# A recommender's GRU kernel: a bf16 count of the sequences alive, and one product that puts the last results in place

## The chip, the cores and the metric

The kernel runs on one core of a Trainium2 chip. The core has five engines that work at the same time, each through its own list of instructions in order: TensorE (PE in the profile; PEld is its loading of weights), VectorE (DVE), ScalarE (ACT), GpSimd (POOL) and SyncE (SP, which here only starts DMAs). They wait for each other through semaphores. TensorE writes to PSUM, which has eight banks; the other data lie in SBUF, in 128 partitions. The metric is the time of one execution on the device in microseconds; a smaller one is better.

## The reference

For B = 1024 sequences of T = 100 steps, with vectors of 128 numbers, the reference computes:

```python
hist_sum = (item_historical_embedding * fmask[:, :, None]).sum(1) / sequential_length[:, None]
_, gru_seq = jax.lax.scan(gru_step, h0, jnp.swapaxes(item_historical_embedding, 0, 1))
keys = jnp.swapaxes(gru_seq, 0, 1)
feat = jnp.concatenate([keys, q, keys - q, q * keys], axis=-1)
score = _mlp(feat, [...], relu)                       # then masked, softmax over the steps
pooled = jnp.einsum('bt,btd->bd', attn, keys)
att_seq = pooled.T[:T]
_, aug_seq = jax.lax.scan(augru_step, h0, (jnp.swapaxes(keys, 0, 1), att_seq))
attention_feature = aug_seq at step sequential_length - 1 of each sequence
comb = [user, item, hist_sum, item * hist_sum, attention_feature]
scores = _mlp(comb, [...], sigmoid)                   # 640 -> 200 -> 80 -> 1
return scores[:, 0]
```

So there are two recurrences of 100 steps, one after the other: a GRU, and a second one (AUGRU) whose update gate is scaled by an attention weight. A sequence needs the second one only as far as its own length.

## The kernel before, in words

**First phase** (`gru_phase`): per step t the two halves of 512 sequences are done one after the other (method `gru`, L577 to L637), then the attention network of the step before (`attend`, L761). Beside this goes a list of small jobs, the generator `load_later`, which moves on by one piece per step, after the gates of that step. It ranks the sequences by length. One of its pieces counts how many sequences are alive at each step: `alive` (L336) is 1 where the length is over the step, as a 128 x 8 x 100 tile, and eight products with a column of ones (L353 to L356) add it up over the partitions into `count`, in PSUM. From `count` VectorE works out `over` (L359 to L370), which chooses between three versions of the second phase with narrower or full widths. The products stand in TensorE's list between the gates of a step and the `attend` of the step before it.

**Second phase** (`augru_phase`): the sequences are sorted by length, so that at step t only the first `widths[t]` columns of each half are worked on (264 at t = 50, 260 at t = 51, 44 at the end). `half_step` (L1279) does one half of one step: products that close the gates with the state (L1268) and open those of the half that follows (L1264), on VectorE the new state and the reset state `r` (L1298, L1300, L1302, L1305, L1308) and the transpose of a key that is needed two steps later (L1253). The two halves alternate, so that one half's VectorE and ScalarE work lies under the other's products. When the width is 72 or less, `whole_step` does both halves at once.

As sequences end, `predict(g)` computes the final network for group g of 128 sorted sequences, in pieces spread over the steps, and writes its 128 results to `early_d` in DRAM with an indirect DMA. The last group, g = 0, ends only at t = 99, so its work is the tail of the kernel, and its results don't go through DRAM. They are put in place by a product: `last_places` (L1505), called once at the end of step t = 50 (`HALF_TIME`, L1582), makes for each of the 128 sequences a row that is 1 at its own index and 0 elsewhere (an iota of 512 and a comparison, twice, both on GpSimd). In the tail four products with the column y repeated 32 times (L1494 to L1502), one for each quarter of the 1024 results, put quarter q on the partitions 32 q to 32 q + 31. VectorE adds this to `all_y` (L1503), which holds the results of the other groups, fetched by `earlier_results` (L1521) from `early_d` and repeated on 32 partitions each. The last DMA (L1630) stores the rows of the partitions 0, 32, 64 and 96.

**What sets the order.** Both phases have a manual schedule: each engine's instructions stand in the order in which the code makes them, and the semaphores follow from the tiles that an instruction reads and writes. A tile that one engine still reads isn't written by another before that read is done, and a tile from a pool with two buffers waits for the readers of the tile two before it. PSUM banks of the second phase are handed out in turn by `bank` (L1176) from a ring of seven.

Of the kernel before, what the change touches and what calls it, by code (L numbers as in the profile page):

```python
# [9 lines left out]
F32 = mybir.dt.float32  # L10
BF16 = mybir.dt.bfloat16
I32 = mybir.dt.int32
U8 = mybir.dt.uint8
AF = mybir.ActivationFunctionType
ALU = mybir.AluOpType
AX = mybir.AxisListType
# [3 lines left out]
P = 128  # L20
B = 1024
T = 100
HB = 512
NH = B // HB
NG = B // P
GH = HB // P

R = 32
# [3 lines left out]
M0, M1 = 200, 80  # L32
# [48 lines left out]
BQ = B // (P // R)  # L81
# [4 lines left out]
def kernel(ctx: ExitStack, tc: tile.TileContext, a: dict, out: bass.AP):  # L86
# [26 lines left out]
    nc = tc.nc  # L113
# [16 lines left out]
    early_d = dram.tile([B, 1], F32, name="early_d")  # L130
# [7 lines left out]
    ident = const.tile([P, P], F32, name="ident")  # L138
    item = const.tile([P, B], F32, name="item")
    hist = const.tile([P, B], F32, name="hist")  # L140
    pooled = const.tile([P, NK, R], F32, name="pooled")
# [1 line left out]
    idx_k = const.tile([P, KH, NH], I32, name="idx_k")  # L143
    quad = const.tile([P, SOON], F32, name="quad")
    used_s = const.tile([P, NH, GH, T - SOON], U8, name="used_s")
    all_y = pooled.rearrange("p k r -> p (k r)")[:, :BQ]
    idx_p = const.tile([P, HB // PR], I32, name="idx_p")
    h_all = const.tile([P, NH, HB], F32, name="h_all")
    h3 = [h_all[:, i, :] for i in range(NH)]
    mid = ctx.enter_context(tc.tile_pool(name="mid", bufs=2))  # L150
# [3 lines left out]
    later = {}  # L154
# [49 lines left out]
    def gru_phase(pools):  # L204
# [11 lines left out]
        pre = pools.enter_context(tc.tile_pool(name="pre", bufs=1))  # L216
# [60 lines left out]
        def load_later():  # L277
# [55 lines left out]
                nc.scalar.copy(room[-1], room_i)  # L333
            yield

            alive = mid.tile([P, NG, T], F32, name="alive", **once)  # L336
            nc.vector.tensor_tensor(
                out=alive,
                in0=length.unsqueeze(2).to_broadcast([P, NG, T]),
                in1=step.unsqueeze(1).to_broadcast([P, NG, T]),  # L340
                op=ALU.is_gt,
            )
            ones = pre.tile([P, 1], F32, name="ones")
            nc.gpsimd.memset(ones, 1.0)
            rlen = pre.tile([P, NG], F32, name="rlen")
            nc.vector.reciprocal(rlen, length)
# [806 lines left out]
    def augru_phase(pools, widths, alive):  # L1153
# [260 lines left out]
        def predict(g, last=False):  # L1414


            m0, m1 = later["m0"], later["m1"]
            n = M0 // MC
            tag = "last" if last else "a"

            def of_pool(name):
                return bank(name) if last else pa.tile([P, HB], F32, tag="a", name=name)


            def rows_of(out_ap, in_ap, o, i):
                nc.gpsimd.indirect_dma_start(
                    out=out_ap,
                    out_offset=o and bass.IndirectOffsetOnAxis(ap=idx_p[:, g : g + 1], axis=0),
                    in_=in_ap,
                    in_offset=i and bass.IndirectOffsetOnAxis(ap=idx_p[:, g : g + 1], axis=0),  # L1430
                )

            part = sp.tile([P, M0], F32, tag=f"part_{tag}", name="part3")
            rows_of(part, part_d, None, True)
            yield
            f0 = sp.tile([MC, n, P], F32, name="f0")
            if last:
                p0 = [of_pool("p0")[:MC, :P] for _ in range(n)]
                for j in range(n):
                    nc.tensor.matmul(  # L1440
                        p0[j], lhsT=part[:, ts(j, MC)], rhs=ident, start=True, stop=False
                    )
                yield
                for j in range(n):
                    nc.tensor.matmul(
                        p0[j].rearrange("p (i r) -> p i r", i=NH),
                        lhsT=m0[:, 4, ts(j, MC)],
                        rhs=h_all[:, :, ts(g, PR)],
                        start=False,
                        stop=True,  # L1450
                    )
            else:
                state = sp.tile([P, NH, PR], F32, name="state3")
                nc.scalar.copy(state, h_all[:, :, ts(g, PR)])
                yield
                p = of_pool("rows")[:, :M0]
                nc.tensor.matmul(
                    p,
                    lhsT=state.rearrange("p i r -> p (i r)"),
                    rhs=m0[:, 4, :],  # L1460
                    start=True,
                    stop=True,
                )
                yield
                nc.vector.tensor_add(part, p, part)
                yield
                p = of_pool("p0")
                p0 = [p[:MC, ts(j, P)] for j in range(n)]
                for j in range(n):
                    nc.tensor.transpose(p0[j], part[:, ts(j, MC)], ident)  # L1470
            yield
            for j in range(n):
                nc.scalar.activation(
                    f0[:, j, :], p0[j], AF.Sigmoid, bias=later["c0"][:, j : j + 1]
                )
            yield
            p1 = of_pool("p1")[:M1, :P]
            for j in range(n):
                nc.tensor.matmul(  # L1479
                    p1, lhsT=m1[:, j, :], rhs=f0[:, j, :], start=(j == 0), stop=(j == n - 1)  # L1480
                )
            yield
            f1 = sp.tile([M1, P], F32, name="f1")
            nc.scalar.activation(f1, p1, AF.Sigmoid, bias=later["c1"])
            yield
            p2 = of_pool("p2")[:, 0:1]
            nc.tensor.matmul(p2, lhsT=f1, rhs=later["m2"], start=True, stop=True)
            yield
            y = sp.tile([P, 1], F32, name="y")
            nc.scalar.activation(y, p2, AF.Sigmoid, bias=later["c2"])  # L1490
            if not last:
                rows_of(early_d, y, True, None)
                return
            p = of_pool("po")[:, :BQ]  # L1494
            for q in range(P // R):
                nc.tensor.matmul(
                    p[ts(q, R), :],
                    lhsT=y.to_broadcast([P, R]),
                    rhs=later["places"][q // 2][:, ts(q % 2, BQ)],
                    start=True,  # L1500
                    stop=True,
                )  # L1502
            nc.vector.tensor_add(all_y, p, all_y)  # L1503

        def last_places():  # L1505
            own = sp.tile([P, 1], F32, name="own3", bufs=1)
            nc.gpsimd.tensor_copy(own, idx_p[:, 0:1])
            later["places"] = []
            for i in range(NH):
                row = wp.tile([P, HB], F32, tag="att_r", name="places", bufs=2)  # L1510
                nc.gpsimd.iota(
                    row,
                    pattern=[[1, HB]],
                    base=i * HB,
                    channel_multiplier=0,
                    allow_small_or_imprecise_dtypes=True,
                )
                nc.gpsimd.tensor_scalar(row, row, own, None, ALU.is_equal)
                later["places"].append(row)

        def earlier_results():  # L1521
            nc.sync.dma_start(
                out=all_y,
                in_=early_d.rearrange("(q c) o -> q (o c)", c=BQ)
                .unsqueeze(1)
                .to_broadcast([P // R, R, BQ]),
            )

        def gathers(q):
# [92 lines left out]
    with none.Else():  # L1622
# [6 lines left out]
                augru(2)  # L1629
    nc.sync.dma_start(  # L1630
        out=out.rearrange("(q c) -> q c", c=BQ),
        in_=all_y.rearrange("(q r) c -> q r c", r=R)[:, 0, :],
    )


# [64 lines left out]
```

## Time and profile before

| | us |
|---|---|
| median of 3 timed runs | 2016.64 (2015.94 to 2016.9) |
| profiled execution, first to last instruction (span) | 1995.2 |
| median less span | 21.4 |
| PE busy in the span | 1980.5 |
| DVE busy | 1673.4 |
| POOL busy | 1262.7 |
| ACT busy | 940.7 |

The profile records one execution with its span; for that execution no other time is given, so its time as a whole is the span and what lies around it, and the median of the timed runs stands beside it. A line of a timeline gives the start and the duration in us, the engine, the line of the kernel, the operation, what is written and read, the shapes, and in brackets how long the engine stood idle before and what ended this. In the lists of groups the last columns are the busy time in us with the mean of one instruction in ns, and the idle time before them. The rows of a view by windows give, for each stretch, its length and the busy time of PE, PEld, DVE, ACT and POOL with the number of instructions, then the clock that TensorE was granted (1.00 is full speed), the DMA engines' busy share and the GB/s. An fp32 product shows as two records on PE and two on PEld.

### The profile page before, as it was taken

The page shows a single profiled execution, that of the slowest core. Times are in us where ns is not written, and L with a number is a line of the kernel's source. Part 1 is how long each engine was busy: PE and PEld are TensorE (multiplying, and loading weights), DVE is VectorE, ACT ScalarE, POOL GpSimd, SP SyncE. Part 2 cuts the span into 40 slices and gives each one's busy share as a digit, 9 for nine tenths or more (in the row PEclk, how much of TensorE's full clock was granted, in tenths as well). Part 3 has the DMA queues.
Part 4 walks back from the last instruction along what each step waited for, and adds up shares of the span by engine and source line. Part 5 has one row for each costly group of instructions (what it writes and reads, how often), then busy time and mean ns, then how long its engine had stood idle before and what let it go on. Part 6 is the DMA issues. An engine that isn't in the chain of part 4 may idle for free.

```text
span 1995.2 us, 40926 instructions
## 1 busy us (share of the span) xinstructions
PE 1980.5 (99%) x15324; PEld 877.7 (44%) x15324; DVE 1673.4 (84%) x3036; ACT 940.7 (47%) x1689; POOL 1262.7 (63%) x1300
## 2 busy tenths in 40 slices
PE   9999999999999999999999999999999999999998
PEld 2333333333333333333333333334444556678997
DVE  7888999887979898888888798998687778888995
ACT  4444454454544444544545444446334444445553
POOL 0333939669796959496796858898763354445331
PEclk9999999999999999999999999999999999999999
DMA  4443333223334434332343333332543333333331
GB/s 125 99 119 92 108 105 102 89 84 108 116 104 113 116 99 134 111 106 85 103 129 108 93 107 108 92 108 67 155 146 92 96 111 97 93 103 100 83 81 35
DMA packets 244572, 205.59 MB, mean 103 GB/s; under 512 B 61811, under 2 KB 207068, under 8 KB 244364
## 3 DMA queue, kind: packets, MB, share of 16 engines
q1 hardware_dynamic: 231852, 170.31, 29.5%
q0 software_dynamic: 12224, 32.05, 5.7%
q8 instruction: 122, 2.00, 0.4%
q14 instruction: 86, 0.70, 0.1%
q10 hardware_dynamic: 288, 0.52, 0.1%
HBM read 146.75 MB, written 54.42 MB: 101 GB/s over the span
## 4 chain that ended last, share of the span: by engine, by line
PE 98%; DVE 1%; ACT 0%; issue 0%; ACTq 0%; DVEq 0%
PE ps L588 51%; PE pm L770 18%; PE ph L1268 5%; PE pr L1264 4%; PE pu L1264 4%; PE ph L1264 4%; PE pu L1268 4%; PE pr L1268 4%; PE last L737 1%; PE pr L1359 0%; PE ph L1359 0%; PE p L1479 0%; ACT pr L1378 0%; PE pd L248 0%; DVE r L1386 0%
## 5 line engine op out<-in xcount | busy, mean ns | idle before, releaser
L588 PE MATMUL ps<-x,wih 128*32 128x512 f32 x4800 | 603.2, 593 | 0.0
L588 PE MATMUL ps<-hn,whh 128*32 128x512 f32 x4752 | 597.1, 592 | 0.0
L588 PEld LDWEIGHTS ps<-x,wih 128*32 128x32 f32 x4800 | 175.6, 110 | 342.7 <-issue 338.1
L588 PEld LDWEIGHTS ps<-hn,whh 128*32 128x32 f32 x4752 | 173.7, 110 | 338.2 <-issue 335.6
L600 ACT ACTIVATE r<-ps,brz 128x512 f32<-128x512 f32 x200 | 137.5, 688 | 381.3 <-PE ps L588 381.1
L573 POOL TENSOR_TENSOR xm<-x,m 128x512 f32<-128x512 f32 x200 | 233.3, 1167 | 66.7 <-DMA m<-mask_d 66.5
L574 POOL TENSOR_TENSOR hist<-hist,xm 128x512 f32<-128x512 f32 x200 | 258.2, 1291 | 15.7
L193 POOL DMA_INDIRECT rows<-keys_d,idx_k x218 | 212.0, 972 | 84.0 <-POOL rows L192 69.2
L700 POOL TENSOR_TENSOR pooled<-pooled,kw 128x512 f32<-128x512 f32 x192 | 245.5, 1279 | 15.1
L699 POOL TENSOR_TENSOR kw<-kt,e 128x512 f32<-128x512 f32 x192 | 206.3, 1074 | 67.9 <-DVE e L888 67.9
L621 ACT ACTIVATE ps<-ps,bih 128x512 f32<-128x512 f32 x198 | 131.1, 662 | 228.4 <-DVE ps L618 228.4
L770 PE MATMUL pm<-hn,wk 128*32 128x512 f32 x1200 | 215.0, 592 | 0.0
L770 PE MATMUL pm<-kq,wkq 128*32 128x512 f32 x1200 | 214.9, 592 | 0.0
L1276 ACT ACTIVATE c<-ph,bh 128x510 f32<-128x510 f32 (+57 forms) x174 | 88.3, 507 | 252.0 <-PE ph L1268 251.5
L608 DVE SCALAR_TENSOR_TENSOR u<-ps,bhh,r 128x512 f32<-128x512 f32 x198 | 147.4, 744 | 68.5 <-PE ps L588 66.3
L770 PE MATMUL pm<-mv,w 128*32 128x512 f32 (+1 forms) x808 | 194.9, 592 | 0.1
L631 DVE TENSOR_TENSOR d<-hn,ps 128x512 f32<-128x512 f32 x198 | 136.0, 687 | 36.0 <-ACT ps L621 35.7
L618 DVE TENSOR_TENSOR ps<-ps,u 128x512 f32<-128x512 f32 x200 | 140.0, 700 | 24.1 <-PE ps L588 3.1
L642 ACT COPY hn<-ps 128x512 f32<-128x512 f32 x198 | 115.4, 583 | 92.5 <-DVE kq L637 90.8
L632 DVE TENSOR_TENSOR d<-ps,d 128x512 f32<-128x512 f32 x198 | 136.9, 691 | 26.2 <-ACT ps L622 11.0
L192 POOL COPY rows<-rest 128x1 f32<-128x1 f32 x186 | 35.0, 188 | 192.8 <-DVE rest L1308 191.1
L1298 DVE TENSOR_TENSOR pu<-pu,c 128x510 f32<-128x510 f32 (+57 forms) x173 | 81.9, 473 | 77.8 <-ACT c L1276 75.5
(271 smaller groups left out, 3138.9 us busy)
## 6 DMA issues: line engine op xcount, KB each, us to landing
x<-in_hist_x SPq DMA_DIRECT2D x210, 256.0 KB
keys_d<-kt SPq DMA_DIRECT2D x48, 1024.0 KB
m<-mask_d SPq DMA_DIRECT2D x200, 128.0 KB
rows<-keys_d,idx_k POOLq DMA_INDIRECT x218, 3.0
s_b<-mv SPq DMA_DIRECT2D x200, 8.0 KB
keys_d<-kt SPq DMA_DIRECT2D x32, 64.0 KB
mask_i<-in_mask SPq DMA_DIRECT2D x8, 200.0 KB
part_d<-part SPq DMA_DIRECT2D x2, 400.0 KB
```

The source lines that it names most:

```text
L193: nc.gpsimd.indirect_dma_start(out=r[:, at, :], out_offset=None, in_=keys_d[q], in_offset=bass.IndirectOffsetOnAxis(ap=idx_k[:, k, i : i + ...
L573: nc.gpsimd.tensor_mul(d, x, m)
L574: nc.gpsimd.tensor_add(acc, acc, d)
L588: nc.tensor.matmul(p[ts(q, R), :], lhsT=w[:, g, ts(q, R)], rhs=v, start=(j == 0), stop=(j == len(parts) - 1),)
L600: nc.scalar.activation(r, pr, AF.Sigmoid, bias=brz[:, 0:1])
L608: nc.vector.scalar_tensor_tensor(out=u, in0=ph, scalar=bhh[:, 2:3], in1=r, op0=ALU.add, op1=ALU.mult,)
L618: nc.vector.tensor_add(pi, pi, u)
L699: eng.tensor_mul(d, k, w)
L700: eng.tensor_add(acc, acc, d)
L770: nc.tensor.matmul(p[i][s, :], lhsT=w[:, s], rhs=v, start=start, stop=stop)
L1264: nc.tensor.matmul(p, lhsT=m[:, 1, :], rhs=k, start=True, stop=False)
L1268: nc.tensor.matmul(p, lhsT=m[:, 0, :], rhs=v, start=False, stop=True)
```

## The change

Two things change. The tile `alive` and the column of ones for the count become bf16. And the last results are placed by one product in place of four. For this, `last_places` makes four rows of 256 instead of two of 512; VectorE takes the maximum of each (1 where the sequence's index lies in that quarter) into a column of `others`, and GpSimd adds the four rows into one, `places`, which is row 0 itself. `others` is then (it - 1) x 1e30: 0 in the sequence's own quarter, -1e30 in the three others. In the tail the product for p2 becomes one of four columns: it is opened with identity x `others` before the last state is known, and closed with the network's last layer in all four columns, so that after the sigmoid y is the result in its own quarter's column and 0 in the others. One product of y (128 x 4) with `places` (128 x 256) gives 4 x 256 results. `all_y` has four partitions in place of 128, and the DMA that fills it and the one that stores it change with it. The order in which the banks go to p1 and p2 of the last group changes, since p2 is now opened first.

```diff
-    all_y = pooled.rearrange("p k r -> p (k r)")[:, :BQ]
+    all_y = pooled.rearrange("p k r -> p (k r)")[: B // BQ, :BQ]
...
-            alive = mid.tile([P, NG, T], F32, name="alive", **once)
+            alive = mid.tile([P, NG, T], BF16, name="alive", **once)
...
-            ones = pre.tile([P, 1], F32, name="ones")
+            ones = pre.tile([P, 1], BF16, name="ones")
...
+                p2 = of_pool("p2")[:, : B // BQ]
+                nc.tensor.matmul(p2, lhsT=ident, rhs=later["others"], start=True, stop=False)
                 yield
...
+            if last:
+                nc.tensor.matmul(
+                    p2,
+                    lhsT=f1,
+                    rhs=later["m2"].to_broadcast([M1, B // BQ]),
+                    start=False,
+                    stop=True,
+                )
+                y = sp.tile([P, B // BQ], F32, name="y4", bufs=1)
+                nc.scalar.activation(y, p2, AF.Sigmoid, bias=later["c2"])
+                p = of_pool("po")[: B // BQ, :BQ]
+                nc.tensor.matmul(p, lhsT=y, rhs=later["places"], start=True, stop=True)
+                nc.vector.tensor_add(all_y, p, all_y)
+                return
...
-            p = of_pool("po")[:, :BQ]
-            for q in range(P // R):
-                nc.tensor.matmul(
-                    p[ts(q, R), :],
-                    lhsT=y.to_broadcast([P, R]),
-                    rhs=later["places"][q // 2][:, ts(q % 2, BQ)],
-                    start=True,
-                    stop=True,
-                )
-            nc.vector.tensor_add(all_y, p, all_y)
...
-            later["places"] = []
-            for i in range(NH):
-                row = wp.tile([P, HB], F32, tag="att_r", name="places", bufs=2)
+            others = later["others"] = sp.tile([P, B // BQ], F32, name="others", bufs=1)
+            places = later["places"] = sp.tile([P, BQ], F32, name="places", bufs=1)
+            for q in range(B // BQ):
+                row = places if q == 0 else wp.tile([P, HB], F32, tag="att_r", name="row3", bufs=2)[:, :BQ]
                 nc.gpsimd.iota(
                     row,
-                    pattern=[[1, HB]],
-                    base=i * HB,
+                    pattern=[[1, BQ]],
+                    base=q * BQ,
                     channel_multiplier=0,
                     allow_small_or_imprecise_dtypes=True,
                 )
                 nc.gpsimd.tensor_scalar(row, row, own, None, ALU.is_equal)
-                later["places"].append(row)
+                nc.vector.tensor_reduce(others[:, q : q + 1], row, AX.X, ALU.max)
+                if q:
+                    nc.gpsimd.tensor_add(places, places, row)
+            nc.vector.tensor_scalar(others, others, 1.0, 1e30, ALU.subtract, ALU.mult)
...
-                in_=early_d.rearrange("(q c) o -> q (o c)", c=BQ)
-                .unsqueeze(1)
-                .to_broadcast([P // R, R, BQ]),
+                in_=early_d.rearrange("(q c) o -> q (o c)", c=BQ),
...
-        in_=all_y.rearrange("(q r) c -> q r c", r=R)[:, 0, :],
+        in_=all_y,
```

More of the change, by code (lines that the diff above doesn't have):

```diff
@@ L1490, in predict @@
             nc.scalar.activation(y, p2, AF.Sigmoid, bias=later["c2"])
-            if not last:
-                rows_of(early_d, y, True, None)
-                return
-            p = of_pool("po")[:, :BQ]
-            for q in range(P // R):
-                nc.tensor.matmul(
-                    p[ts(q, R), :],
-                    lhsT=y.to_broadcast([P, R]),
-                    rhs=later["places"][q // 2][:, ts(q % 2, BQ)],
-                    start=True,
-                    stop=True,
-                )
-            nc.vector.tensor_add(all_y, p, all_y)
+            rows_of(early_d, y, True, None)
         def last_places():
```

## The prediction

> **What bounds the kernel now.** I read the page first, then the windows by stage, then the chain around the three places that the diff touches.
>
> ```profile
> span 1995.2 us, 40926 instructions
> PE 1980.5 (99%) x15324; PEld 877.7 (44%) x15324; DVE 1673.4 (84%) x3036; ACT 940.7 (47%) x1689; POOL 1262.7 (63%) x1300
> PE 98%; DVE 1%; ACT 0%; issue 0%; ACTq 0%; DVEq 0%
> ```
>
> TensorE is busy for 99% of the span, and 98% of the chain that ended last lies on it. So time that the change takes off TensorE counts in full, and so does time in which it makes TensorE wait. The span is 1995.2 us; the median of the timed runs is 2016.64 us, so 21.4 us lie outside the span. The change touches nothing there, and I add the sum to the median. About 0.2%, 4.0 us here, is what a measurement of this kernel can tell from no change: over 2020.67 is slower, under 2012.6 faster.
>
> **The count.** The chain and the waits there:
>
> ```profile
> 119.94 1.27 PE count L354 x15
> 121.21 0.26 issue
> 121.47 0.25 PE count L354
> DVE ps L618 <- PE ps L588: 3.1, 1, 3.1
> ```
>
> Eight fp32 products show as 16 records and hold the chain for 1.27 + 0.26 + 0.25 = 1.78 us. The trace has no bf16 product. Cost from above: as now, no gain. From below: one record per product and each shorter. The pitch of the records is (1.27 + 0.25 - 0.25) / 15 = 0.085 us; one record in place of two leaves 8 x 0.085 = 0.68 and takes away 0.68; if the gap of 0.26 goes too and the passes are shorter still, up to 1.35 goes. But the last row is a warning: VectorE waited 3.1 us for a product of L588 that stands in the records as long ended, it was let go at the same moment at which the last count product started, and TensorE itself stood still for 0.26 us just before. If that stall ends at a moment that TensorE does not set, a shorter count only waits longer for it, and the gain is some 0.05 us. I take 0.7, with 0.05 and 1.35 as ends. The comparison that writes bf16 in place of fp32 stays one VectorE instruction of the same 800 elements, off the chain: nothing.
>
> **The masks for the last results.** This is the part that costs. Before, GpSimd makes them alone, far ahead of its readers. VectorE and GpSimd around the place:
>
> ```profile
> 1803.22 0.20 POOL L1507 CAST own<-idx_p 128x1 f32<-128x1 int32 x1
> 1803.37 0.57 POOL L1511 IOTA places<- 128x512 f32 x1
> 1804.04 1.58 POOL L1518 TENSOR_SCALAR places<-places,own 128x512 f32<-128x512 f32 x1
> ...
> 1816.41 0.45 DVE L1253 STREAM_TRANSPOSE k<-rows 128x256 f32<-128x256 f32 x1
> 1817.11 0.44 DVE L1298 TENSOR_TENSOR pu<-pu,c 128x264 f32<-128x264 f32 x1 [0.26 <-ACT c L1276]
> 1817.52 0.43 DVE L1300 TENSOR_TENSOR r<-h_all,pr 128x260 f32<-128x260 f32 x1
> ...
> 1818.15 0.60 PE L1264 MATMUL pu<-k,wu 128*128 128x260 f32 x2
> 1818.37 0.41 PEld L1268 LDWEIGHTS ph<-r,wh 128*128 128x128 f32 x2
> 1818.59 0.60 PE L1268 MATMUL ph<-r,wh 128*128 128x260 f32 x2
> ```
>
> The call stands after step t = 50, whose width of 264 dates it: VectorE ends that step with L1253 at 1816.86, and the next instruction is that of t = 51 (width 260 in L1300). GpSimd is there at 1803.22, 13.6 us earlier. In the changed kernel VectorE gets four maxima over rows that GpSimd makes, and one small instruction, between L1253 and L1298. The two engines are tied both ways. Row 0 is the tile `places` itself: GpSimd's first add writes into it, so it must wait for VectorE's first maximum. GpSimd can therefore make rows 0 and 1 ahead, and then stands until 1816.9. From there rows 2 and 3 are made while VectorE, which works in order, holds the whole recurrence behind its third and fourth maximum. (Row 3 also waits for the buffer of row 1, which is free by then.)
>
> Prices, from the nearest rows:
>
> ```profile
> L1511 POOL IOTA places<- 128x512 f32 x2 | 1.1, 568 | 0.0
> L308 POOL IOTA step_i<- 128x100 int32 x1 | 0.2, 206 | 0.0
> L1518 POOL TENSOR_SCALAR places<-places,own 128x512 f32<-128x512 f32 x2 | 3.1, 1574 | 0.2
> L1585 POOL TENSOR_SCALAR minus<-wr 128x128 f32<-128x128 f32 x1 | 0.5, 535 | 0.0
> L700 POOL TENSOR_TENSOR pooled<-pooled,kw 128x448 f32<-128x448 f32 x2 | 2.3, 1136 | 0.2
> L684 POOL TENSOR_TENSOR pooled<-pooled,kw 128x64 f32<-128x64 f32 x1 | 0.3, 317 | 0.1
> L873 DVE TENSOR_REDUCE top<-e 128x32 f32<-128x256 f32 x10 | 4.2, 420 | 0.3
> L446 DVE TENSOR_SCALAR quad<-kc_f x4: 142/143/144, 440.7 to 440.9; 128x1 f32<-128x1 f32 x4
> ```
>
> At 256 elements, on the line between the two sizes: iota 0.34 (and 0.10 until the comparison starts, as from 1803.94 to 1804.04), comparison 0.88, add 0.73; maximum 0.42, last instruction 0.15. From 1816.86: maximum 0.42, signal 0.06, add 0.73, iota 0.44, comparison 0.88, add 0.73, iota 0.44, comparison 0.88, signal 0.05, maximum 0.42, last 0.15 = 5.20 us. VectorE is free at 1822.06, where L1298 began at 1817.11: 4.95 us late. L1300 ended at 1817.95, TensorE took its weights at 1818.37, so 0.42 us of that is slack, and TensorE stands for 4.5 us. Low end: halves of the 512 prices (0.28 and 0.79), 0.65 for the add, 0.25 for the maximum, no gaps, slack up to the product itself (0.64): 3.2. High end: 0.1 us more between GpSimd's instructions: 5.2. Nothing gives this back: TensorE has no other work queued there, and 99% busy leaves no reserve. The third add and the two `minus` copies behind it end about 1824; the next gathers wait for the recurrence anyhow.
>
> The Trainium skill (GPSIMD Engine Reference, Performance versus the Vector engine) says that an operation with one input runs at 1.03 cycles an element, by which the two comparisons would be an estimated 0.4 us each and the stall about 3.5 us. The row of 1574 ns for 512 elements is three times that, and I go by the row.
>
> **The clock behind the gap.** What the profile says of TensorE's clock after a gap:
>
> ```profile
> 1406.34:1409.76 3.42, 0.59 (x3) 0.15 (x2) 3.18 (x6) 0.00 (x0) 2.66 (x4) 1.00 0.60 112
> 1409.76:1413.17 3.41, 3.41 (x5) 1.36 (x6) 3.27 (x6) 0.00 (x0) 2.50 (x4) 0.50 0.43 118
> 1986.61:1990.03 3.42, 1.88 (x11) 1.20 (x10) 0.50 (x2) 1.28 (x5) 0.00 (x0) 1.00 0.06 23
> 1990.03:1993.44 3.41, 1.08 (x8) 0.20 (x8) 0.42 (x1) 0.00 (x0) 0.00 (x0) 0.50 0.05 13
> ```
>
> A stretch of 3.4 us with 0.59 us of TensorE work was followed by 3.4 us at a granted clock of 0.50, and so was one with 1.88 us. These stretches lie on one grid (1409.76 + 170 x 3.4133 = 1990.03). A gap of 4.5 us leaves at least 2.2 us of one stretch empty wherever the grid lies, so about 1.2 us of work in it, less than the 1.88 above: I expect one stretch at half clock, which costs half of the part of it that TensorE works in. Where the gap fills the later stretch that is 3.41 / 2 = 1.7; where it reaches into the slow stretch, down to 0.6. I take 1.3, with 0 and 1.7 as ends.
>
> The Trainium skill (TensorE: Matmul & The Clock Gate, HAM oscillation) asks for a whole idle window of some 3.4 us. By it the gap would hold a full stretch in about three of ten positions of the grid, the mean cost would be near 0.5, and the sum 0.8 lower. The stretch with 1.88 us of work speaks against it, so I keep 1.3.
>
> **The tail.**
>
> ```profile
> PEld p L1445 <- DVE h_all L1592: 0.8, 1, 0.8
> 1989.34 0.40 PE p L1487 x2
> 1989.76 0.27 ACT y L1490
> 1990.07 1.13 PE po L1496 x8
> 1991.22 0.42 DVE pooled L1503
> ...
> L1496 PE MATMUL po<-places,y x8: 634/635/636, 1990.1 to 1990.5; 128*32 128x256 f32 x8
> 1984.58 0.57 SPq L1522 DMA_DIRECT2D pooled<-early_d  x1
> ```
>
> The opening product (identity by four columns) goes in ahead of L1445. Its nearest row is L1487, 0.40 for a full weight load and one column; the loads idle there for 0.8 us until h_all comes, so it costs nothing, and at most 0.4 if that cover were gone. L1487 and L1490 take four columns for one: nothing. The placing product: its eight records, of 0.635 us each, fit into 1.13, so the four column groups already ran side by side, two deep. One full product of two records by 256 columns is two deep as well: at the clock of 0.50 twice the 0.44 pitch of the product at 1818.15, and some 0.2 to drain, 1.08. No gain; if that moment falls into full clock, 0.5 less. The add is 256 elements deep on 4 partitions as on 128: 0.42. The earlier results come in with 4 KB in place of 128 KB, on SP's queue, issued at 1984.58, over 6 us ahead of the add: hidden before and after. The last store moves the same 4 KB. Tail: 0, ends -0.5 and +0.4.
>
> **Sum.** +4.5 (stall) + 1.3 (clock) - 0.7 (count) + 0 (tail) = +5.1: 2016.64 + 5.1 = **2021.7 us**.
>
> **The rivals.** (1) The stall comes and the clock holds: +4.5 - 0.7 = +3.8, 2020.4. For it speaks that only two slow stretches can be seen, both with a tail or a change of phase around them; against it, that the gap here is emptier than one of them. 0.22. (2) No stall, the time not slower: GpSimd's whole work on the masks is 0.20 + 4 x (0.44 + 0.88) + 3 x 0.73 = 7.7 us, less than its lead of 13.6. If the first add need not wait for the first maximum, all rows are ready when VectorE comes, which then loses 4 x 0.42 + 0.15 = 1.8 less its 0.3 of idle time and the 0.42 of slack: +1.1 - 0.7, 2017.0. This turns on that one wait; the diff has both instructions on the same tile, so 0.09. (3) The stall is longer: a second stretch at half clock (+1.7), or the signals between VectorE and GpSimd cost more than 0.06: 2023.4 and over. 0.09. (4) The count gains nothing because TensorE is held to 121.43 either way: a part of the forecast's own range, +0.65, 2022.3.
>
> **How the numbers follow.** Forecast 0.60, rivals 0.22, 0.09, 0.09. The lowest sum with a stall is 3.2 + 0 - 1.35 - 0.1 = +1.75, 2018.4; the highest that I keep is 5.2 + 1.7 - 0.05 - 0.1 = +6.75, 2023.4; beyond lie rival 2 and most of rival 3, under 2 in 10. Slower needs over +4.0: most of the forecast (its own range is +2.9 to +6.8), a third of rival 1 and all of rival 3, 0.64. Within 0.2%: the rest of the forecast and rival 1, and rival 2, 0.34. Faster would need 4 us, for which no term is large enough: 0.02.
>
> **What would show it.** In the new profile: on VectorE, two maxima back to back after the L1253 of t = 50 and then two that wait for GpSimd about 1.6 us each or more; on GpSimd, a wait of some 11 us ahead of the first add; on TensorE a gap of about 4.5 us ahead of an L1268 of width 260, and behind it a stretch of 3.4 us at a clock of 0.50; eight records in the count; the tail from L1445 to the add as long as before. No such gap, or a total at or under 2017, would make the forecast wrong, and so would a gap that the following steps give back.

## The result and the profile after

Five runs of the changed kernel took 2020.6 to 2024.88 us, median 2024.37; five runs of the kernel before beside them 2015.94 to 2018.39, median 2016.9. The ratio is 1.0033, with a 95% interval of 1.0021 to 1.0044: slower by 4.2 to 8.9 us. The forecast was 2021.7 with a range up to 2023.4, so the direction was right and the size too small.

The profile after is of the run of 2020.6, the shortest of the five. From its page, the span, the engines and the chain:

```profile
span 2018.8 us, 40913 instructions
PE 1985.3 (98%) x15312; PEld 936.5 (46%) x15312; DVE 1674.7 (83%) x3041; ACT 941.9 (47%) x1689; POOL 1271.0 (63%) x1307
PE 94%; DVE 2%; POOL 1%; issue 1%; DMA 1%; ACT 1%; POOLq 0%; DVEq 0%; ACTq 0%
```

Only 2020.6 - 2018.8 = 1.8 us lie outside the span, not 21.4. The span is 23.6 us longer than that of before, but the change made only a part of that, as the next sections show.

**The masks.** The timeline around them (columns as before):

```profile
1828.86 0.45 DVE L1253 STREAM_TRANSPOSE k<-rows 128x256 f32<-128x256 f32 x1
1829.23 0.38 DVE L1524 TENSOR_REDUCE others<-places 128x1 f32<-128x256 f32 x1
1829.53 0.40 DVE L1524 TENSOR_REDUCE others<-row 128x1 f32<-128x256 f32 x1
1829.76 0.73 POOL L1526 TENSOR_TENSOR places<-places,row 128x256 f32<-128x256 f32 x1 [11.19 <-DVE others L1524]
...
1831.84 0.42 DVE L1524 TENSOR_REDUCE others<-row 128x1 f32<-128x256 f32 x1 [1.90 <-POOL row L1523]
...
1833.96 0.42 DVE L1524 TENSOR_REDUCE others<-row 128x1 f32<-128x256 f32 x1 [1.71 <-POOL row L1523]
...
1834.42 0.34 DVE L1527 TENSOR_SCALAR others<-others 128x4 f32<-128x4 f32 x1
1834.67 0.43 DVE L1298 TENSOR_TENSOR pu<-pu,c 128x264 f32<-128x264 f32 x1
...
1835.48 1.23 PE L1268 MATMUL ph<-r,wh 128*128 128x260 f32 x2 [4.28 <-DVE r L1300]
...
1841.42 0.48 ACT L1276 ACTIVATE c<-ph,bh 128x260 f32<-128x260 f32 x1 [2.43 <-PE ph L1268]
```

GpSimd stood 11.19 us for the first maximum; the third and fourth maximum waited 1.90 and 1.71 us for GpSimd's rows. From L1253 to L1298 it is 1834.67 - 1828.86 = 5.81 us, where it was 1817.11 - 1816.41 = 0.70 before: VectorE is 5.11 us late, and TensorE stands for 4.28 us. The product after it takes 1.23 us instead of 0.60.

A measure for the whole place is used below, the *step at the masks*: how much more an execution is shifted against the first profile of before at a ScalarE instruction L1276 behind the gap than at the L1253 ahead of the maxima. It is taken at the second L1276 behind the gap. In the first profile L1253 stands at 1816.41, and L1276 here:

```profile
1821.83 0.48 ACT L1276 ACTIVATE c<-ph,bh 128x260 f32<-128x260 f32 x1 [1.21 <-PE ph L1268]
```

So after: (1841.42 - 1821.83) - (1828.86 - 1816.41) = 19.59 - 12.45 = 7.14 us.

**The clock.** The windows on the grid of 3.4133 us, around that gap (length, busy time of PE, PEld, DVE, ACT, POOL, granted clock, DMA share, GB/s):

```profile
1830.53:1833.94 3.41, 0.67 (x4) 0.24 (x2) 0.42 (x1) 0.00 (x0) 3.12 (x5) 1.00 0.04 10
1833.94:1837.36 3.42, 1.88 (x4) 1.51 (x5) 2.99 (x9) 0.48 (x1) 1.92 (x4) 0.50 0.03 9
1837.36:1840.77 3.41, 3.41 (x9) 2.70 (x8) 2.32 (x6) 0.90 (x2) 2.41 (x4) 0.50 0.25 74
1840.77:1844.18 3.41, 3.41 (x17) 3.02 (x16) 2.21 (x6) 1.51 (x4) 2.10 (x3) 1.00 0.46 130
```

Two stretches at half clock followed, not one. The first of them still holds the end of the gap, and the second is full of work at half speed. Their cost is half of the work in them, (1.88 + 3.41) / 2 = 2.6 us.

**The count.** The chain there:

```profile
118.83 0.30 PE count L354 x7
119.13 0.91 PE pm L770 x5
120.03 0.25 issue
120.28 2.93 PE pm L770 x24
```

Eight records, and 0.30 us on the chain where there were 1.78. But TensorE stands for 0.25 us a little later, among the products of the attention network, and ScalarE waited 2.4 us there ("ACT ps L622 <- remote"; "remote" is a release that the profile can't put down to an instruction). At 106 us this execution was 1.11 us ahead of the first profile of before, behind the count 1.55, so 0.44 of the 1.48 stayed.

**The tail.**

```profile
2010.36 0.28 PE L1444 MATMUL p<-others,ident 128*128 128x4 f32 x2
...
2011.07 0.68 PE L1447 MATMUL p<-h_all,m 128*100 128x128 f32 x4 [0.42 <-DVE h_all L1598]
...
2013.57 0.26 ACT L1497 ACTIVATE y<-p,c 128x4 f32<-128x4 f32 x1 [0.47 <-PE p L1489]
2013.88 0.59 PE L1499 MATMUL po<-places,y 128*4 128x256 f32 x2 [0.35 <-ACT y L1497]
2014.52 0.41 DVE L1500 TENSOR_TENSOR pooled<-po,pooled 4x256 f32<-4x256 f32 x1 [3.50 <-PE po L1499]
```

From L1447 to y it is 2.50 us, as it was (1989.76 - 1987.26). The opening product lies in idle time. The placing product took 0.59 at full clock; the four before it took 1.08 at half clock. In the count alone (below), whose old tail ran at full clock, they took 0.64, so nearly all of that difference is the clock.

**What the change did not make.** The second phase starts with a stall that the first profile of before doesn't have (windows again):

```profile
1434.59:1438.00 3.41, 1.91 (x5) 0.57 (x3) 0.00 (x0) 0.00 (x0) 2.50 (x4) 1.00 0.34 96
1438.00:1441.41 3.41, 0.00 (x0) 0.00 (x0) 0.00 (x0) 0.04 (x1) 2.50 (x4) 1.00 0.35 105
1441.41:1444.83 3.42, 0.00 (x0) 0.00 (x0) 0.00 (x0) 0.53 (x1) 2.68 (x3) 0.50 0.41 115
```

TensorE, VectorE and ScalarE stand together for about 10 us, waiting for nothing that the profile shows (a wait of VectorE of 14.0 us is marked "issue"), and some 16 us are lost with the slow clock behind it. The experiments show that this goes with the chip and not with the change: kernels without the change have it too.

### The profile page after: what moved, and what is told of

It is laid out like the page before. It is cut to its first block, busy times and chain, and to the rows that moved or that the text cites. A ratio compares the mean times of both kernels' runs of the same rounds, so it can differ in the third digit from the quotient of the medians.

```text
span 2018.8 us, 40913 instructions
## 1 busy us (share of the span) xinstructions
PE 1985.3 (98%) x15312; PEld 936.5 (46%) x15312; DVE 1674.7 (83%) x3041; ACT 941.9 (47%) x1689; POOL 1271.0 (63%) x1307
## 4 chain that ended last, share of the span: by engine, by line
PE 94%; DVE 2%; POOL 1%; issue 1%; DMA 1%; ACT 1%; POOLq 0%; DVEq 0%; ACTq 0%
PE ps L588 50%; PE pm L770 17%; PE ph L1268 4%; PE pu L1264 4%; PE pr L1268 4%; PE pu L1268 4%; PE ph L1264 4%; PE pr L1264 4%; DMA rows<-keys_d,idx_k 1%; POOL rows L193 0%; PE pr L1359 0%; PE last L737 0%; PE ph L1359 0%; POOL att_r L158 0%; PE p L1481 0%
## 5 line engine op out<-in xcount | busy, mean ns | idle before, releaser
L588 PE MATMUL ps<-x,wih 128*32 128x512 f32 x4800 | 758.5, 592 | 0.0
L588 PE MATMUL ps<-hn,whh 128*32 128x512 f32 x4752 | 753.2, 592 | 0.0
L588 PEld LDWEIGHTS ps<-x,wih 128*32 128x32 f32 x4800 | 224.7, 110 | 322.2 <-issue 280.5
L588 PEld LDWEIGHTS ps<-hn,whh 128*32 128x32 f32 x4752 | 222.8, 110 | 315.5 <-issue 299.3
L770 PE MATMUL pm<-hn,wk 128*32 128x512 f32 x1200 | 252.4, 592 | 0.0
L770 PE MATMUL pm<-kq,wkq 128*32 128x512 f32 x1200 | 252.3, 592 | 0.0
L770 PE MATMUL pm<-mv,w 128*32 128x512 f32 (+1 forms) x808 | 233.6, 592 | 0.8 <-DVE e L869 0.5
L1276 ACT ACTIVATE c<-ph,bh 128x510 f32<-128x510 f32 (+57 forms) x174 | 88.3, 507 | 261.4 <-PE ph L1268 229.7
L1298 DVE TENSOR_TENSOR pu<-pu,c 128x510 f32<-128x510 f32 (+57 forms) x173 | 81.8, 473 | 91.7 <-ACT c L1276 73.0
```

The lines of the kernel that those rows point to most:

```text
L588: nc.tensor.matmul(p[ts(q, R), :], lhsT=w[:, g, ts(q, R)], rhs=v, start=(j == 0), stop=(j == len(parts) - 1),)
L770: nc.tensor.matmul(p[i][s, :], lhsT=w[:, s], rhs=v, start=start, stop=stop)
```

## The experiments

Kernels that are told of as one group ran on one chip, beside runs of before on that chip.

**Before, a second profile.** Unchanged.

> The kernel before, unchanged, for a second profile. My theory: the first profile caught a short execution (1995.2 us against a median of 2016.64); an ordinary one has a span of about 2015, with the stall of some 16 us at the start of the second phase that the changed kernel's profile shows near 1431 us, and only 1.8 us lie outside the span. Rival: the span is 1995 again and 21 us lie outside it.

```profile
span 1995.3 us, 40926 instructions
```

Measured: 1997.08 us, again 1.8 outside the span. Before's median was 1995.63 on this chip (23 runs). So my theory had the 1.8 right and the span wrong: on this chip the stall at the start of the second phase doesn't come. In the five groups, that of the result counted, before's median was 2016.9 and 2018.2 in two and 1995.6, 1996.0 and 1996.5 in three. The changed kernel's first profile and all four profiles of the group at 2018.2 have the stall near 1435 us, those of the three don't. The first profile of before (1995.2) fits the three and its times (2016.64) the two, so they seem to come from different chips, which is not shown. Differences below are within a group.

**The count alone, and the placing alone.**

```diff
 count_only:  before, with
-            alive = mid.tile([P, NG, T], F32, name="alive", **once)
+            alive = mid.tile([P, NG, T], BF16, name="alive", **once)
 (and ones in BF16)
 place_only:  the changed kernel with both in F32
```

> The kernel before with the bf16 count alone. My theory (the cost of the change lies in the masks): 0.4 to 0.7 us less than before, so about 2016.3 and the same within what can be measured; eight records of about 0.21 us in the count, and the stall of 1.8 us or so that TensorE had behind it now stands among the products of pm. Rival (the bf16 product brings a wait of its own, or moves the start of the recurrence): 2 us or more above before.

> The changed kernel with the count as it was, in fp32. My theory: the whole cost is here, about 7 us above before (the changed kernel's +6.7 and the 0.4 that the count gave), about 2024: TensorE stands for 4.3 us ahead of an L1268 of width 260, and one or two stretches of 3.4 us at half clock follow. Rival (the cost comes from both parts together, or from the count): at most 3 us above before.

Measured: the count alone 1996.55 against 1995.63, ratio 1.0002 (0.9993 to 1.0011); the placing alone 2001.68, ratio 1.0028 (1.0017 to 1.0040), +6.1 between the medians. The whole loss comes from the placing. For the count alone the interval is -1.4 to +2.2 us: the times can't tell the expected -0.4 to -0.7 from nothing. Its chain:

```profile
119.47 0.29 PE count L354 x7
119.77 0.91 PE pm L770 x5
120.67 1.36 issue
122.03 1.97 PE pm L770 x15
```

The count holds the chain for 0.29 in place of 1.78, and TensorE then stands 1.36 us: nearly all of the gain is gone again within 3 us.

The placing alone, windows from the gap on:

```profile
1819.75:1823.17 3.42, 0.00 (x0) 0.00 (x0) 1.38 (x4) 0.00 (x0) 3.15 (x6) 1.00 0.00 0
1823.17:1826.58 3.41, 2.89 (x7) 2.31 (x8) 2.64 (x8) 0.93 (x2) 1.97 (x4) 0.50 0.12 34
1826.58:1829.99 3.41, 3.41 (x18) 3.01 (x17) 2.75 (x8) 1.77 (x4) 2.17 (x5) 1.00 0.45 84
```

The same gap of 4.28 us, but here it covers one stretch fully and little of the next, and only one stretch is slow. The step at the masks is 5.95 us. By the work in the slow stretch it is 2.89 / 2 = 1.45 for the clock, so 4.5 for the gap.

**The changed kernel again.**

> The changed kernel, unchanged, for a second profile and more times. My theory: TensorE's gap of 4.28 us again, and behind it one stretch at half clock or two, as the gap lies on the grid of stretches (two if the stretch in which it begins holds under some 1.4 us of work, one if more): 4.6 + 1.7 to 4.6 + 2.9, so 6.3 to 7.5 us above before, less nothing for the count. Rival (the times above that come from a second place in the span): 8 us or more above before, with a difference that does not arise at the masks.

Measured: 2001.43 against 1996.02, ratio 1.0028 (1.0018 to 1.0037). The gap is 4.26 us and the step at the masks 7.29, with two slow stretches:

```profile
1818.21:1821.62 3.41, 0.36 (x2) 0.00 (x0) 0.72 (x2) 0.00 (x0) 3.11 (x5) 1.00 0.01 2
1821.62:1825.03 3.41, 2.20 (x5) 1.81 (x6) 3.00 (x9) 0.54 (x2) 1.97 (x5) 0.50 0.05 17
1825.03:1828.45 3.42, 3.42 (x9) 2.71 (x9) 2.01 (x6) 0.85 (x2) 2.17 (x5) 0.50 0.27 78
```

(2.20 + 3.42) / 2 = 2.8 for the clock leaves 4.5 for the gap again.

**The gap filled.** The changed kernel, with products that nothing reads:

```diff
                     half_step(t, i)
+                    if (t, i) == (HALF_TIME + 1, 0):
+                        fill = pa.tile([P, HB], F32, tag="a", name="fill")
+                        for _ in range(9):
+                            nc.tensor.matmul(fill[:, : 2 * P], lhsT=ident,
+                                rhs=wh.rearrange("p k m -> p (k m)"), start=True, stop=True)
```

> The changed kernel with nine products more, identity by 256 columns of weights into a bank that nothing reads, that TensorE has to do while it waits behind step 51's first half; they take about 9 x 0.435 = 3.9 of the 4.3 us. My theory (the gap costs its length, and one or two stretches at half clock after it cost 1.7 each): the wait stays, the half clock goes, 4.3 us above before, so about 2 us under the changed kernel (which was 5.7 to 6.7 above). Rival (the clock's part is something else, for instance the gathers that come late): 6 us above before, as without the nine products.

Measured: 2022.32 against 2018.21, ratio 1.0018 (1.0009 to 1.0027). The windows:

```profile
1832.66:1836.07 3.41, 3.41 (x18) 2.96 (x17) 1.50 (x5) 1.34 (x3) 2.20 (x4) 1.00 0.14 38
1836.07:1839.49 3.42, 3.02 (x15) 2.33 (x13) 1.68 (x6) 0.00 (x0) 3.24 (x6) 1.00 0.00 0
1839.49:1842.90 3.41, 3.41 (x16) 3.00 (x17) 3.34 (x10) 1.48 (x4) 1.70 (x5) 1.00 0.13 39
```

VectorE waits as long as before, the clock holds, and the step at the masks is 4.55 us (+4.1 in the times). This is the gap alone; what the clock costs is 5.95 - 4.55 = 1.4 with one slow stretch, 7.14 - 4.55 = 2.6 and 7.29 - 4.55 = 2.7 with two. All three agree with half of the work in the slow stretches.

**The tie between the engines undone.** Four rows in tiles of their own, their sum in another, the maxima last:

```diff
-            for q in range(B // BQ):
-                row = places if q == 0 else wp.tile(...)
+            rows = []
+            for i in range(NH):
+                row = wp.tile([P, HB], F32, tag="att_r", name="row3", bufs=2)
+                for q in range(2):
+                    part = row[:, ts(q, BQ)]
...
+            nc.gpsimd.tensor_add(places, rows[0], rows[1])
+            for row in rows[2:]:
+                nc.gpsimd.tensor_add(places, places, row)
+            for q, row in enumerate(rows):
                 nc.vector.tensor_reduce(others[:, q : q + 1], row, AX.X, ALU.max)
```

> The changed kernel, but the four mask rows lie in tiles of their own, and the sum of them in another: GpSimd waits for VectorE nowhere, and VectorE's four maxima come behind all of them. My theory (the tie both ways makes the stall): GpSimd needs about 7.6 us and is there some 11 us ahead, so all is ready when VectorE ends step 50; VectorE loses four maxima at a pitch of 0.30 and one small instruction, less its idle time of 0.3, some 1.2 us, TensorE stands for about 0.8 us, and no stretch at half clock follows: +0.8 - 0.4, about 2017 and the same as before. Rival (the amount of work that GpSimd has, or the maxima themselves, make the stall): TensorE stands for 3 us or more again, about 2021 to 2024.

Measured: 1995.96 against 1995.63, ratio 1.0001 (0.9992 to 1.0011). The timeline:

```profile
1815.96 1.35 DVE L1532 TENSOR_REDUCE others<-row 128x1 f32<-128x256 f32 x4
1817.35 0.17 DVE L1533 TENSOR_SCALAR others<-others 128x4 f32<-128x4 f32 x1
...
1818.24 0.70 PE L1268 MATMUL ph<-r,wh 128*128 128x260 f32 x2 [0.31 <-DVE r L1300]
```

The same work on both engines, but nobody waits: GpSimd had its rows and their sum done at 1810.2. TensorE stands 0.31 us, the step at the masks is 0.57, and the clock holds.

**GpSimd alone.** Columns from four comparisons of one index each, one mask of 256 from the index less its quarter's start, no work for VectorE:

```diff
+                nc.gpsimd.tensor_scalar(above[:, q : q + 1], own, float(q * BQ), None, ALU.is_ge)
...
+            nc.gpsimd.tensor_sub(others, above[:, : B // BQ], above[:, 1:])
...
-                nc.vector.tensor_reduce(others[:, q : q + 1], row, AX.X, ALU.max)
```

> The changed kernel, but GpSimd makes both the four columns and the mask alone, from four comparisons of one column and one row of 256, and VectorE has no work in it. My theory (the cost is VectorE's wait for GpSimd alone): no gap ahead of the L1268 of width 260, no stretch at half clock there, the time of before within 1 us; the count's gain is swallowed by the stall behind it and the placing by one product gives at most 0.5. Rival (the new tail or the new opening product costs something that the gap hid): 2 us or more above before.

Measured: 2017.43 against 2018.21, ratio 0.9995 (0.9986 to 1.0004). The step at the masks is 0.00. The new tail, present here, costs nothing that can be measured.

**A gap made on purpose in the kernel before.** Maxima on VectorE at the same place, 18 or 9, into a cell that nothing reads:

```diff
                 last_places()
+                scrap = sp.tile([P, 1], F32, name="scrap", bufs=1)
+                for _ in range(18):   # or 9
+                    nc.vector.tensor_reduce(scrap, wh.rearrange("p k m -> p (k m)"), AX.X, ALU.max)
```

> The kernel before, masks by GpSimd as they were, and 18 maxima over 256 columns of weights on VectorE, which nothing reads, where the changed kernel has its four: 18 x 0.30 less 0.3 of idle time, 5.1 us late. My theory (a gap on TensorE of this length costs the same whatever fills VectorE): a gap of 4.4 to 4.7 us and one or two stretches of 3.4 us at half clock, 6.1 to 8.0 us above before. Rival (it is the two engines' tie, GpSimd's late work behind it, that costs beyond the gap): 4.5 above before.

> The kernel before with 9 of those maxima: VectorE 9 x 0.30 - 0.3 = 2.4 us late, a gap of 2.0 us on TensorE. My theory (a stretch of 3.4 us in which TensorE works no more than some 1.9 us is followed by one at half clock): it depends on where the gap lies on the grid of stretches, so 2.0 above before in some executions and 3.7 in others. Rival (only a whole empty stretch lets the clock fall, as the Trainium skill has it in TensorE: Matmul & The Clock Gate, HAM oscillation): 2.0 above before in all executions, no stretch at half clock.

Measured: 18 maxima 2028.57 against 2018.21, ratio 1.0050 (1.0034 to 1.0065); 9 maxima 2021.27, ratio 1.0020 (1.0011 to 1.0030), with runs from 2018.53 to 2026.32. My price for them was off: written into one cell they took 8.10 / 18 = 0.45 us each, not 0.30, so the gaps were 6.85 and 2.77 us. The long one had two slow stretches and a step of 9.45, with GpSimd uninvolved. That the tie adds nothing beyond its gap is borne out: (1.34 + 3.41) / 2 = 2.4 for the clock, as in these windows, leaves 7.1 for the gap.

```profile
1837.22:1840.64 3.42, 0.00 (x0) 0.00 (x0) 3.16 (x8) 0.00 (x0) 0.00 (x0) 1.00 0.00 0
1840.64:1844.05 3.41, 1.34 (x3) 1.15 (x4) 3.30 (x9) 0.07 (x1) 0.18 (x1) 0.50 0.00 0
1844.05:1847.46 3.41, 3.41 (x9) 2.68 (x9) 2.47 (x7) 1.31 (x3) 2.39 (x4) 0.50 0.27 75
```

The short one fell across two stretches, and in the profiled execution the clock held; its step is 3.03:

```profile
1831.90:1835.32 3.42, 1.67 (x8) 1.11 (x6) 3.15 (x9) 0.85 (x2) 0.00 (x0) 1.00 0.14 37
1835.32:1838.73 3.41, 2.40 (x11) 2.13 (x12) 3.38 (x11) 1.34 (x3) 0.70 (x2) 1.00 0.07 20
1838.73:1842.14 3.41, 3.41 (x18) 3.01 (x17) 3.08 (x10) 1.32 (x3) 2.85 (x5) 1.00 0.45 119
```

The stretch with 1.67 us kept the clock, so the 1.9 us of my theory is too high a bound; whether only an empty stretch lets the clock fall this profile doesn't decide. Two rows of GpSimd alone, further on in the same phase, do: a stretch with 1.45 us of work is not empty, and the next one is slow.

```profile
1974.36:1977.77 3.41, 1.45 (x12) 1.30 (x12) 1.75 (x9) 0.68 (x4) 1.90 (x2) 1.00 0.52 119
1977.77:1981.18 3.41, 3.41 (x18) 3.41 (x17) 1.81 (x7) 1.10 (x4) 0.00 (x0) 0.50 0.16 39
```

**The count away from the stall.** Two kernels, each before with the bf16 count: in one the count is two pieces of work later, in the other the store of `rlen_d` (1024 single numbers of 4 bytes) stands behind the count.

```diff
 count_later:
             nc.sync.dma_start(out=len_r, in_=a["len_i"].partition_broadcast(P))
             yield
+            yield
+            yield
 rlen_later:
-            nc.sync.dma_start(out=rlen_d.rearrange("g p -> p g"), in_=rlen)
...
             nc.sync.dma_start(out=over_d, in_=over_i)
             yield
+            nc.sync.dma_start(out=rlen_d.rearrange("g p -> p g"), in_=rlen)
+            yield
```

> The kernel before with the bf16 count, and the count itself two pieces of work later, while the 4-byte store and the broadcast stay where they are. My theory (the stall is not the count's; it ends 10.5 to 12 us after the 4-byte store was issued, whatever TensorE has queued, and swallows what is gained ahead of it): engines stall at the same distance from the store, now with products of the recurrence in it, and the count, away from it, takes 0.68 less than in fp32: 0 to 1 us under before, the same within what can be measured. Rival (the count makes the stall): the stall moves with the count.

> The kernel before with the bf16 count, the 4-byte store moved behind the count, the broadcast left ahead of it. My theory (the 4-byte store makes the stall): no stall of 1 us or more ahead of or behind the count; it stands 10.5 to 12 us behind the store's new place; the time of before within 1 us. Rival (the broadcast of the lengths, 4 KB to each of 128 partitions' rows, makes it): the stall stays at the count.

Measured: count_later 1997.57 against 1996.02, ratio 1.0009 (1.0000 to 1.0018); rlen_later 1994.33, ratio 0.9995 (0.9986 to 1.0004). In count_later ScalarE's wait of 2.5 us stayed where it was, ending 11.7 us after the store's issue (121.20 - 109.50), though the count had gone to 146 us: the count doesn't make the stall. The gain that I expected did not come in the times. The profile stood 2.4 us ahead of the first profile of before at 127 us (1.24 of it at 106 us already); it lost 0.8 between 200 and 300 us and 1.6 near 710 us, and why stays open. In rlen_later the chain has no stall at the count:

```profile
116.80 3.00 PE ps L589 x28
119.80 0.29 PE count L353 x7
120.09 3.48 PE pm L771 x30
```

At 127 us it is 1.57 us ahead of the first profile of before, 0.14 of it at 106 us already. My theory expected the stall behind the store's new place, at 140 us; none of 1 us is there. The edit also moved the broadcast of the lengths: no longer behind the store in SyncE's list, it was issued at 102.40 us, where in before it was 111.11, 0.43 behind the store. So no such wait follows the store alone or the broadcast alone at these places, and which of the two, or which moment, it takes stays open.

What the traces do show is that the transfers stand. In before SyncE issued loads from 114.38 us on, yet the DMA engines moved only 15 GB/s between 113 and 121 us, in rlen_later 202. In the twelve traces with the store ahead of the count SyncE took 5.3 to 6.5 us for one issue of the mask `m` in this stretch, in the two others 0.4. Behind the store's new place SyncE issues nothing from 130.7 to 140.8 us, so nothing could stand there. How standing transfers hold up a compute engine is not shown.

No run moves the store with the fp32 count, so the 1.43 us are not divided between the shorter count and the absent stall.

**Both mended.** GpSimd alone, and the store behind the count.

> The changed kernel with GpSimd making the columns and the mask alone, and with the 4-byte store behind the count. My theory: no gap at the masks and no stall at the count, so the bf16 count gives its 1.1 (0.68 for the pitch, the rest the gap that stood ahead of the last record): 1 us under before, 5 to 7 under the changed kernel; a difference of 0.05% to before that the times may not tell from none. Rival (one of the two mendings works only without the other): 2 us or more above before.

Measured: 1994.25 against 1996.53, ratio 0.9991 (0.9982 to 1.0000): -2.3 us to before, where the changed kernel was +5.4 in another group. It is 1.65 us ahead of the first profile of before at 127 us (0.22 of it at 106 us already) and 1.47 at the masks, with a step of 0.00 there. Against before itself, 0.09% is at the edge of what the times can tell.

## Why the prediction was too low

**The stall: right.** Forecast 4.95 us late for VectorE and 4.5 on TensorE; measured 5.11 and 4.28 idle, 4.55 with what follows (the gap filled). Its cause, the two-way tie, is shown: the same instructions without the tie cost 0.57. The rivals without a stall fall with it, and so does rival 1, in which the clock holds. The comparisons took 0.92 to 0.95 us at 256 elements, 0.88 by the line between the rows. The estimate of 0.4 from the Trainium skill (GPSIMD Engine Reference, Performance versus the Vector engine) is not borne out by the trace.

**The clock: the step that failed.** The prediction put it as "I expect one stretch at half clock, which costs half of the part of it that TensorE works in", 1.3 us. What was missing is that the slow stretch is itself judged. In the rows above, stretches at full clock with 0.00, 0.36, 0.67 and 1.45 us of work were followed by a slow one, those with 1.67 and 1.91 were not. Of the slow stretches, those with 1.34, 1.88 and 2.20 us of work were followed by another slow one, that with 2.89 was not. Every whole stretch of the fourteen traces fits two bounds. At full clock up to 1.45 us of work were followed by a slow stretch and 1.50 or more were not, the last 10 us of each run aside. Of the slow stretches up to 2.61 us were followed by another and 2.82 or more were not; at half clock that is 1.3 to 1.4 us of full-speed work.

A gap of 4.28 us is 0.87 longer than a stretch. If it begins early in a stretch, with little work ahead of it, it reaches so far into the next that this one, slow, stays under its bound, and a second follows. In the placing alone it began 0.34 us before a stretch, and the slow one behind it held enough. So the term is 1.4 or 2.6 to 2.7, by where the grid lies. By the two bounds (an estimate) one slow stretch follows when the gap begins 0.3 to 1.9 us ahead of a boundary, about half of the positions, and two otherwise.

The 1.88 that the prediction used as its bound came from the last microseconds of the kernel. There stretches with 1.7 to 2.2 us of busy time were followed by one at half clock in twelve traces, where elsewhere such stretches kept the clock, so it doesn't carry over. Why the tail differs is not shown.

The Trainium skill (TensorE: Matmul & The Clock Gate, The HAM clock gate) has the free-running window of 3413 ns, and the traces agree: the two slow stretches of before lie 170 x 3.4133 us apart. It has the clock fall after an idle window; the stretches with 0.67 and 1.45 us of work disagree.

Rival 3 named this case, "a second stretch at half clock (+1.7)", with a chance of 0.09; what was measured lies in it.

**The count: mis-sized.** Forecast -0.7; the times alone, 1.0002, don't decide it, but the profiles do. Between 106 and 123 us, against the first profile of before, the other four with the fp32 count there lost 0.3 to 0.7 us. The six with the bf16 count in the same place ran from 0.6 lost to 0.4 gained: on the mean some 0.15 us better than the five in fp32, and less than they differ among themselves. The warning was in the text, a stall whose end TensorE doesn't set, and this is what happened: the wait ended 10.5 to 12.3 us behind the store's issue in all of them. So rival 4, the count that gains nothing, came true beside the forecast. With the store moved, both profiles gained 1.43 us at that place.

**The tail: right**, at 0 within its ends: from y to the end of the last addition it is 1.36 us at full clock in the new form and 1.44 in the old.

**What lies outside the span: wrong, without effect on the sum.** I took 21.4 us for it. It is 1.8; the rest is, as far as the groups show, the difference between two chips. The sum was added to the median, so it stood.

With the measured sizes the sum is 4.55 + 2.6 + 0 + 0 = +7.2, so 2023.8; between the medians it was 2024.37 - 2016.9 = +7.5. That the two are so close is in part luck: the very execution whose step is 7.14 took only 2020.6 - 2016.9 = 3.7 us more than before's median. In two other groups it was +6.1 for the placing alone and +5.4 for the whole change. The spread among the runs of one kernel, 4.3 us in the five of after, is larger than the step between one slow stretch and two (1.2 us). Slow stretches elsewhere (near 1410 and 1980 us, in some executions) add to it; how much each does was not separated.

## What to carry to other kernels

When work is moved to a second engine beside a recurrence, look for a tile that both write or read in turn: there the lead of the first engine is lost, and all that it has still to do lies on the path. Give each row its own place and let the second engine come last. In these traces a gap on TensorE that left one 3.4-us stretch with less than about 1.5 us of work cost more than its length: add half of the work in each slow stretch, and ask of the slow stretch, too, whether it holds enough work to bring full clock back. A gain just ahead of a stall whose end TensorE doesn't set can be worth nothing until that stall is moved.

## What was not expected of the hardware

- The same program took about 1996 us in three groups and 2017 to 2018 in two; some 16 us of the difference are one stall of TensorE, VectorE and ScalarE at the start of the second phase, marked "issue", with a slow clock behind it. Its cause was not looked for.
- Where a store of 1024 single numbers of 4 bytes was followed by a broadcast, one compute engine waited 2.4 to 3.8 us, until 10.5 to 12.3 us after the store was issued, in all twelve traces. With the fp32 count it was VectorE, in three of five for a product that had ended by the records; with bf16 it was ScalarE, for a release that the profile doesn't name. With the two apart (two traces) the wait is gone.
- Maxima over 256 columns followed each other at 0.30 us on VectorE where each had its own output column, and at 0.45 where all wrote the same one. The latter also read weights instead of the masks, so the cause is not separated.
